# Convolution rows loaded once and copied shifted, with the background work drawn in sequence, in a four-layer network kernel

## The chip, the cores and the metric

The kernel runs on one core of a Trainium2 chip. The metric is device time in microseconds (us), the median of three executions. One further view, the profile, is of a single execution. Everything is f32.

The engines are named as in the profile: PE is TensorE's matmul side and PEld its weight load, DVE is VectorE, ACT is ScalarE, POOL is GpSimd, SP is SyncE. POOL, SP and ACT also issue DMA transfers, each on a queue of its own; sixteen DMA engines carry them all.

## The reference

The input x has shape 8 x 384 x 32 x 32 (images, channels, height, width). Four layers follow each other, all on the same shape.

- Layer 0: RMS norm over channels; a selective scan ("mamba") over the 1024 pixels of an image, forwards and backwards, on 384 channels with 16 states each; the gated result is projected and added, scaled, to x plus a local 3x3 depthwise branch with a sigmoid gate.
- Layer 1: a residual block with batch norm, a 1x1, a depthwise 3x3 and a 1x1 convolution; linear attention with 8 heads; layer norm and an MLP of 384 to 1536 to 384 with GELU.
- Layer 2: seven depthwise convolutions up to 13x13, some dilated, each with batch norm, summed.
- Layer 3: a 1x1 convolution with a residual, then a 13x13 depthwise convolution with batch norm plus a one-weight branch, and GELU.

The recurrence at the centre of layer 0 is

```
h[t] = exp(delta[t] * A) * h[t-1] + delta[t] * u[t] * B[t]      (per channel and state)
y[t] = sum over states of h[t] * C[t], plus D * u[t]
```

The seven kernels of layer 2 are merged into one 13x13 kernel per channel, and layer 3's last convolution is one 13x13 kernel too; both are computed by matmuls against Toeplitz matrices.

## The kernel before, in words

**Layers 0 and 1** work image by image. For each image b there are three generators, each of which issues a piece of work and then yields a number, its cost:

- `front(b)` (L554): norm, input projection (`in`, stored through `uz` tiles to `u_d` and `z_d`), local branch (`lc`), causal 1-D convolution (`c`, through `ut` loads), and the softplus that makes `dl` and `v` (Abs, Relu, Exp, Ln on ScalarE, sums on VectorE), written to DRAM for the scan.
- `scan(b)` (L678): 48 units, one for each direction, half image, group of 128 channels and group of 4 states. In a unit, ScalarE makes `da` by four exponentials (L754, two buffers), VectorE multiplies (`du`, L767, four buffers), runs the recurrence as one scan instruction (L774 or L777), and multiplies by C in the next unit (L691). PE then sums over states into `acc` (L693). After three channel groups of the backward direction the output projection (`op`) follows.
- `layer1(b)` (L840): the residual block (`h`, `dw`, `c2`), attention (`kv`, `q`, `rzb`, `pj`), norm, and the MLP (`mf`, GELU into `hm`, `mo`).

The main loop (L1036) runs `scan(b)`, and after each unit draws background work: `front(b + 1)`, `layer1(b - 1)`, and for the first two images preparations of weights (`fold`, L793, in image 0; `prepare`, L830, in image 1). It draws from whichever generator has the smallest drawn share of its declared total (108, 310, 30, 64), so that all of them advance side by side, and it draws until the drawn cost keeps pace with the units done. What is left after the last unit follows.

`prepare` merges the convolution kernels (L169) and expands them, with 64 DRAM to DRAM transfers on the POOL queue (L239, `tp_d<-g_d`, 672 KB each), into Toeplitz form; each pair of transfers is a step of cost 2.

The order of instructions on an engine isn't quite that of the program text. A scheduling framework places each instruction when its inputs and buffers are there in its own reckoning, by program order where several are ready, and fixes the queues of all engines before the kernel runs. Each engine then takes its queue in order. Tiles come from pools with a fixed number of buffers per tag: `t2` (128x512, 11 buffers), `s2` (128x512, 3, for the scan's small tiles), `a6` (128x3x512, 7), `w` (weights, 4), `im` (6), `bct` (4), `da` (2), `du` (4). PSUM has three `mm` tiles for short results, three `mo` for long ones, two `acc`.

**Layers 2 and 3** come when all images are done. `conv` (L282) treats the eight images of a channel row by row: a row of all images lies in DRAM with padding zeros between the images (`PADW`, 12; length `RL`, 364). For every four groups of four channels it loads the rows twice into `xt` (two buffers), into partitions 0 to 63 and, one element further, into 64 to 127 (L290 to L295), so that a matmul of 128 rows takes two taps at once. Each group has 28 matmul instructions (56 PE passes of half width) on PSUM tiles of six buffers. The Toeplitz tiles `tp` come by SP and ACT DMAs (L299 to L305) into three buffers. `put2` copies results out on VectorE and ScalarE by turns; between the two convolutions a 1x1 layer (L336 to L357) writes the padded rows of layer 3; `put3` applies GELU and stores the output.

Of the kernel before, what the change touches and what calls it, by code (L numbers as in the profile page):

```python
# [37 lines left out]
N_A6, N_T2, N_S2, N_W, N_IM = 7, 11, 3, 4, 6  # L38
TP = H * (KP // 2)
PADW = KS - 1  # L40
# [23 lines left out]
def tile_layers(  # L64
# [39 lines left out]
    RL = PADW + B * (W + PADW)  # L104
# [58 lines left out]
    def kernels(small, large):  # L163
# [65 lines left out]
        for g_d, t_d in ((g2_d, tp2_d), (g3_d, tp3_d)):  # L229
            for at in range(0, C // 2, NP):  # L230
                for q in range(2):
# [8 lines left out]
                    yield 2  # L240
# [8 lines left out]
    XL = RL - PADW // 2 - 6  # L249
    with tc.tile_pool(name="cw", bufs=1) as cwp, tc.tile_pool(name="cx", bufs=2) as cxp, tc.tile_pool(  # L250
# [31 lines left out]
        def conv(t_d, src_d, tag, put):  # L282
# [3 lines left out]
            xt = tp = None  # L286
            for g in range(NQ):
                if g % GB == 0:
                    xt = cxp.tile([P, 2 * GB, XL], FP, tag="xt", name=f"xt_{tag}_{g}")
                    for q in range(2):  # L290
                        src = bass.AP(
                            src_d.tensor, src_d[4 * g, 0, PADW - KS // 2 + q].offset,
                            [[RL, 2 * H], [2 * H * RL, 2 * GB], [1, XL]],
                        )
                        nc.gpsimd.dma_start(xt[2 * H * q : 2 * H * (q + 1)], src)  # L295
                ps = cps.tile([P, HALF], FP, tag="cv", name=f"cv_{tag}_{g}")
                if g % (GB // 2) == 0:
                    tp = toep[g // (GB // 2) % len(toep)]
                    for q in range(2):  # L299
                        for e in range(2):  # L300
                            lo = 2 * H * q + H * e
                            (nc.scalar if e else nc.sync).dma_start(
                                tp[lo : lo + H, :, e].rearrange("p g j t -> p g (j t)"),
# [32 lines left out]
        for t in range(H // 2):  # L336
# [3 lines left out]
            for m in range(NC):  # L340
# [10 lines left out]
                for r in range(2):  # L351
                    mid = xo[:, m, r, PADW:RL].rearrange("p (b w) -> p b w", w=W + PADW)[:, :, 0:W]
# [18 lines left out]
def _layers01(tc, nc, B, xv, x2_d, dram, ident, mean_w, eps5, eps6, one, half, minus1, vec, bns, bnt,  # L371
# [12 lines left out]
    with ExitStack() as ctx:  # L384
# [48 lines left out]
        zero = wp.tile([P, C + NC + 1], FP, tag="zero", name="zero")  # L433
        nc.gpsimd.memset(zero, 0.0)
        for i in range(2):
            for t, n in ((xn_d, IMG), (u_d, UL), (h_d, IMG)):
                pads = t[i].rearrange("(c p) i -> p c i", p=P)
                for c in range(NC):
                    for a in range(0, n, C):
                        e = min(n, a + C)  # L440
                        nc.gpsimd.dma_start(pads[:, c, a:e], zero[:, 0 : e - a])
# [21 lines left out]
        def s2(name):  # L463
            return sp.tile([P, HALF], FP, tag="s2", name=name, bufs=N_S2)

# [15 lines left out]
        def defer(n, fn):  # L481
            e = [n, fn]
            late.append(e)
            return e

        def force(e):
            if e in late:
                late.remove(e)
                e[1]()
# [64 lines left out]
        def front(b):  # L554
# [22 lines left out]
            for e in range(2):  # L577
                w = wtile(inproj_t[:, e * C : (e + 1) * C], f"win_{b}_{e}")
                for h in range(2):
                    for m in range(NC):  # L580
                        ps = psum(f"in_{b}_{e}_{m}_{h}")
                        dense(ps, w, m, xn[h])
                        t = t2(f"uz_{b}_{e}_{h}_{m}")
                        if e == 0:
                            nc.scalar.copy(t, ps)
                            nc.gpsimd.dma_start(uo[:, m, 3 + h * HALF : 3 + (h + 1) * HALF], t)
                        else:
                            nc.scalar.activation(t, ps, AF.Silu)  # L588
# [565 lines left out]
```

## Time and profile before

| what | us |
| --- | --- |
| median of 3 executions (6063.13 to 6068.56) | 6067.35 |
| the profiled execution's own time | 6068.56 |
| its span | 6066.8 |
| PE busy | 4850.3 (80%) |
| DVE busy | 3998.1 (66%) |
| ACT busy | 2852.0 (47%) |
| POOL busy | 1216.0 (20%) |
| start to the first scan multiply | 242.8 |
| scan of image 0 | 478.9 |
| scan of image 1 | 739.8 |
| scan of image 2 | 707.8 |
| scans of images 3, 4, 5, 6 | 556.5, 553.4, 550.6, 557.1 |
| scan of image 7 | 486.4 |
| layer 1 of image 7 alone | 391.8 |
| layers 2 and 3 | 801.6 |

A scan's stretch runs from its first L767 multiply to that of the next image. The page of the profile shows busy time per engine, the span in 40 slices with digits for tenths of busy time, the costliest groups of instructions with their mean duration and what ended the idle time ahead of them, and DMA issues. Other views answer for a stretch of time: busy time by engine, or who waited for whom.

### The profile page before, as it was taken

To read this page: it belongs to the slowest core of one execution; us is meant where nothing else is said; L and a number is where in the kernel's file an instruction comes from. 1 tells how busy PE (TensorE), PEld (TensorE's weight loads), DVE (VectorE), ACT (ScalarE), POOL (GpSimd) and SP (SyncE) were. 2 spreads that over 40 slices of the span, in tenths; PEclk is the share of its full clock that TensorE was granted. 3 is DMA by queue.
4 is the path that set the end of the run, shared out by engine and by line. 5 is a ranking of instruction groups with operands and counts; after the bars stand their busy time and mean duration, and the time that the engine had idled before them with its cause. 6 is when DMAs were issued, how large, how long until landed. Compare 5 with 4: busy or idle time off the path is not lost. (4 is left out here: it accounts for less than half of the span.)

```text
span 6066.8 us, 53234 instructions
## 1 busy us (share of the span) xinstructions
PE 4850.3 (80%) x19054; PEld 2142.6 (35%) x19054; DVE 3998.1 (66%) x2768; ACT 2852.0 (47%) x3941; POOL 1216.0 (20%) x1953
## 2 busy tenths in 40 slices
PE   3665546675479989898998999898978879798899
PEld 1121112222124324232333333242323324497488
DVE  0499995565674897998899789978989921000200
ACT  1555433443435755684577467556735513000211
POOL 4211111222122221212121121211110010211133
PEclk8676767787789989898999899898989979899999
DMA  8655554556473664567457556755663431598799
GB/s 284 202 181 178 181 187 135 167 171 186 139 224 117 192 203 147 170 203 211 143 181 212 157 183 184 213 151 165 199 171 111 142 95 47 111 221 192 220 217 196
DMA packets 429276, 1060.29 MB, mean 175 GB/s; under 512 B 61500, under 2 KB 111908, under 8 KB 429012
## 3 DMA queue, kind: packets, MB, share of 16 engines
q0 software_dynamic: 188640, 679.21, 39.0%
q1 hardware_dynamic: 210704, 354.31, 18.8%
q10 hardware_dynamic: 29668, 23.36, 1.6%
q8 instruction: 151, 2.47, 0.2%
q14 instruction: 113, 0.93, 0.1%
HBM read 807.16 MB, written 293.47 MB: 181 GB/s over the span
## 5 line engine op out<-in xcount | busy, mean ns | idle before, releaser
L754 ACT ACTIVATE da<-dlt,neg_a 128x512 f32<-128x512 f32 x1536 | 1005.2, 713 | 1061.3 <-DVE du L774 570.3
L767 DVE TENSOR_TENSOR du<-vr,bct 128x2048 f32<-128x2048 f32 x384 | 875.2, 2284 | 46.9 <-DMA vr<-v_d 41.0
L691 DVE TENSOR_TENSOR du<-du,bct 128x2048 f32<-128x2048 f32 x384 | 877.2, 2286 | 4.1 <-DVE xx L972 0.3
L777 DVE TENSOR_TENSOR_SCAN du<-da,du 128x2052 f32<-128x2052 f32 x192 | 848.8, 4427 | 13.9 <-ACT da L754 8.5
L774 DVE TENSOR_TENSOR_SCAN du<-da,du 128x2052 f32<-128x2052 f32 x192 | 848.0, 4426 | 8.5 <-ACT da L754 5.6
L693 PE MATMUL acc<-du,selt 128*32 128x512 f32 x3072 | 570.9, 687 | 324.2 <-DVE du L691 308.4
L1008 PE MATMUL mo<-hm,w 128*128 128x512 f32 x1152 | 568.0, 634 | 130.4 <-ACT hm L1006 129.3
L500 PE MATMUL mf<-ln,w 128*128 128x512 f32 x1152 | 552.3, 617 | 36.9 <-DMA w<-w_d 36.9
L1008 PEld LDWEIGHTS mo<-hm,w 128*128 128x128 f32 x1152 | 218.5, 200 | 474.8 <-issue 236.3
L500 PEld LDWEIGHTS mf<-ln,w 128*128 128x128 f32 x1152 | 214.9, 195 | 365.8 <-issue 326.2
L693 PEld LDWEIGHTS acc<-du,selt 128*32 128x32 f32 x3072 | 92.5, 115 | 681.8 <-DVE du L691 403.8
L312 PE MATMUL cv_b<-xt_b,toep 128*64 128x256 f32 x2688 | 304.5, 387 | 34.7 <-DMA xt_b<-xp_d 16.9
L509 PE MATMUL dw<-dw_i,t3b 96*32 96x512 f32 x1152 | 252.3, 784 | 99.0 <-DMA dw_i<-h_d 87.8
L312 PE MATMUL cv_a<-xt_a,toep 128*64 128x256 f32 x2688 | 302.9, 386 | 30.1 <-issue 24.2
L312 PEld LDWEIGHTS cv_b<-xt_b,toep 128*64 128x64 f32 x2688 | 291.6, 195 | 48.1 <-issue 33.5
L500 PE MATMUL in<-xn,win 128*128 128x512 f32 x576 | 284.2, 628 | 28.8 <-ACT uz L588 22.6
L312 PEld LDWEIGHTS cv_a<-xt_a,toep 128*64 128x64 f32 x2688 | 291.6, 195 | 41.1 <-issue 39.6
L754 ACT ACT_TABLE_LOAD x195 | 250.2, 1283 | 67.3 <-DVE du L777 41.1
L509 PE MATMUL lc<-lc_i,t 96*32 96x512 f32 x1152 | 188.4, 671 | 65.0 <-DMA lc_i<-xn_d 64.2
L1006 ACT ACTIVATE hm<-mf,biasf 128x512 f32<-128x512 f32 x192 | 129.9, 686 | 225.7 <-PE mf L500 224.3
L327 DVE COPY yt<-cv_a 128x256 f32<-128x256 f32 x48 | 20.4, 425 | 309.6 <-PE cv_a L312 309.6
L500 PE MATMUL h<-xx,c 128*128 128x512 f32 x288 | 143.6, 659 | 81.3 <-DMA xx<-x_d 81.3
(212 smaller groups left out, 6353.9 us busy)
## 6 DMA issues: line engine op xcount, KB each, us to landing
dlt<-dl_d SPq DMA_DIRECT2D x384, 256.0 KB, 5.3
vr<-v_d SPq DMA_DIRECT2D x384, 256.0 KB, 5.4
bct<-bc_d SPq DMA_DIRECT2D x256, 256.0 KB, 4.0
ut<-u_d POOLq DMA_DIRECT2D x192, 257.5 KB, 4.7
lc_i<-xn_d POOLq DMA_DIRECT2D x192, 228.8 KB, 4.6
dw_i<-h_d POOLq DMA_DIRECT2D x192, 228.8 KB, 4.2
tp_d<-g_d POOLq DMA_DIRECT2D x64, 672.0 KB, 9.4
w<-w_d POOLq DMA_DIRECT2D x64, 576.0 KB, 5.1
```

The lines of the kernel that those rows point to most:

```text
L312: nc.tensor.matmul(ps[2 * H * e : 2 * H * (e + 1), 0:BW], tp[:, 2 * (g % (GB // 2)) + e, :, :, t].rearrange("p c j -> p (c j)"), rhs, star ...
L327: nc.vector.tensor_copy(hold["t"][:, g % GB, :], ps)
L500: nc.tensor.matmul(ps, w[:, k, m * P : (m + 1) * P], rhs[k] if isinstance(rhs, list) else rhs[:, k, :], start=(k == 0), stop=(k == NC - 1),)
L509: nc.tensor.matmul(ps[32 * j : 32 * j + 32, :], lhs(j, i), rhs(j, i), start=(i == 0), stop=(i == taps - 1), skip_group_check=True,)
L691: nc.vector.tensor_mul(dv, dv, cct[:, 1:2, :].to_broadcast([P, 4, HALF]))
L693: nc.tensor.matmul(acc[32 * j : 32 * j + 32, :], selt, dv[:, j, :], start=False, stop=(r == NR - 1), skip_group_check=True,)
L754: nc.scalar.activation(da[:, SEG * j + 1 : SEG * (j + 1)], dlt[:, j, :], AF.Exp, scale=neg_a[:, 4 * c + j, r : r + 1],)
L767: nc.vector.tensor_mul(flat(1)[:, :, 0:HALF], vt, bct[r][:, 0:1, :].to_broadcast([P, 4, HALF]))
L774: nc.vector.tensor_tensor_scan(du[:, s], da[:, s], du[:, s], 0.0, ALU.mult, ALU.add)
L777: nc.vector.tensor_tensor_scan(du[:, s][:, ::-1], da[:, s][:, ::-1], du[:, s][:, ::-1], 0.0, ALU.mult, ALU.add)
L1006: nc.scalar.activation(hm, ps, AF.Gelu, bias=biasf[:, NC * i + f, :])
L1008: nc.tensor.matmul(acc[m], wb[:, f, m * P : (m + 1) * P], hm, start=(i == 0 and f == 0), stop=(i == FF // C - 1 and f == NC - 1),)
```

## The change

The diff has these parts.

1. In `conv`, the rows are loaded once, into one half of the partitions, and VectorE copies them, shifted by one element, into the other half. `flip` alternates which half is loaded, from one load to the next, and the Toeplitz tile's halves are placed to match.
2. `PADW` is 6 in place of 12, and `RL` 312 in place of 364. Two more elements stand at the end of a row.
3. The main loop draws from one sequence: all of `front(b + 1)`, then `fold` (image 0), then `layer1(b - 1)`. The declared totals are 94, 30 and 290, and the pace is counted over 48 steps in place of 47.
4. `prepare` is gone: its work is the end of `fold`, and the Toeplitz steps have cost 0.
5. `s2` is gone, its tiles come from `t2`, which has 10 buffers; `w` has 5 buffers and `bct` 5.
6. `uz`, `xr` and `fr` are `a6` tiles of three chunks, with one transfer each for three.
7. The residual of layer 1 is deferred by 0 in place of 1 steps, without the call that forces it ahead of the attention.
8. The tile of zeros is 512 wide in place of 388, so that the padding fills take 54 issues in place of 66.

```diff
-N_A6, N_T2, N_S2, N_W, N_IM = 7, 11, 3, 4, 6
+N_A6, N_T2, N_W, N_IM = 7, 10, 5, 6
-PADW = KS - 1
+PADW = KS // 2
-    RL = PADW + B * (W + PADW)
+    RL = PADW + B * (W + PADW) + 2
...
-                    yield 2
+                    yield 0
...
-    XL = RL - PADW // 2 - 6
+    XL = RL - 1
...
-                    for q in range(2):
-                        src = bass.AP(
-                            src_d.tensor, src_d[4 * g, 0, PADW - KS // 2 + q].offset,
-                            [[RL, 2 * H], [2 * H * RL, 2 * GB], [1, XL]],
-                        )
-                        nc.gpsimd.dma_start(xt[2 * H * q : 2 * H * (q + 1)], src)
+                    flip = g // GB % 2
+                    src = bass.AP(
+                        src_d.tensor, src_d[4 * g, 0, 0].offset,
+                        [[RL, 2 * H], [2 * H * RL, 2 * GB], [1, XL]],
+                    )
+                    half0, half1 = (xt[2 * H * e : 2 * H * (e + 1)] for e in (flip, 1 - flip))
+                    nc.gpsimd.dma_start(half0, src)
+                    nc.vector.tensor_copy(half1[:, :, 0 : XL - 1], half0[:, :, 1:XL])
...
+                            to = 2 * H * (q ^ flip) + H * e
                             (nc.scalar if e else nc.sync).dma_start(
-                                tp[lo : lo + H, :, e].rearrange("p g j t -> p g (j t)"),
+                                tp[to : to + H, :, e].rearrange("p g j t -> p g (j t)"),
...
-        zero = wp.tile([P, C + NC + 1], FP, tag="zero", name="zero")
+        zero = wp.tile([P, HALF], FP, tag="zero", name="zero")
...
                 for h in range(2):
+                    t = a6(f"uz_{b}_{e}_{h}")
                     for m in range(NC):
                         ps = psum(f"in_{b}_{e}_{m}_{h}")
                         dense(ps, w, m, xn[h])
-                        t = t2(f"uz_{b}_{e}_{h}_{m}")
                         if e == 0:
-                            nc.scalar.copy(t, ps)
-                            nc.gpsimd.dma_start(uo[:, m, 3 + h * HALF : 3 + (h + 1) * HALF], t)
+                            nc.scalar.copy(t[:, m, :], ps)
...
+                    if e == 0:
+                        nc.gpsimd.dma_start(uo[:, :, 3 + h * HALF : 3 + (h + 1) * HALF], t)
+                    else:
+                        nc.gpsimd.dma_start(zv[b][:, :, bass.ts(h, HALF)], t)
...
-                        t = sp.tile([P, 2, HALF], FP, tag="bct", name=f"bct_{b}_{d}_{h}_{e}", bufs=4)
+                        t = sp.tile([P, 2, HALF], FP, tag="bct", name=f"bct_{b}_{d}_{h}_{e}", bufs=5)
...
-        def prepare():
             large = lambda name: sp.tile([P, NC * C], FP, tag="w", name=name, bufs=N_W)
             yield from kernels(t2, large)
...
-                    res[h].append(defer(1, residual))
+                    defer(0, residual)
...
-                work.append([front(b + 1), 108, 0])
+                work.append((front(b + 1), 94))
+            if b == 0:
+                work.append((fold(), 30))
             if b > 0:
-                work.append([layer1(b - 1), 310, 0])
-            if b == 0:
-                work.append([fold(), 30, 0])
-            if b == 1:
-                work.append([prepare(), 64, 0])
-            need = sum(n for _, n, _ in work)
+                work.append((layer1(b - 1), 290))
+            need = sum(n for _, n in work)
+            steps = (cost for g, _ in work for cost in g)
             done = 0
             for i, _ in enumerate(scan(b)):
                 tick()
-
-                while work and done < need * (i + 1) / (rounds - 1):
-                    w = min(work, key=lambda w: w[2] / w[1])
-                    cost = next(w[0], None)
+                while done < need * (i + 1) / rounds:
+                    cost = next(steps, None)
                     if cost is None:
-                        work.remove(w)
-                        continue
-                    w[2] += cost
+                        break
                     done += cost
-            for w in work:
-                for _ in w[0]:
-                    tick()
+            for _ in steps:
+                tick()
```

## The prediction

> **What bounds the kernel now.** I began with the page's slices and its cost table, to see which engines are full and when.
>
> ```profile
> PE   3665546675479989898998999898978879798899
> DVE  0499995565674897998899789978989921000200
> PEclk8676767787789989898999899898989979899999
> DMA  8655554556473664567457556755663431598799
> L754 ACT ACTIVATE da<-dlt,neg_a 128x512 f32<-128x512 f32 x1536 | 1005.2, 713 | 1061.3 <-DVE du L774 570.3
> L767 DVE TENSOR_TENSOR du<-vr,bct 128x2048 f32<-128x2048 f32 x384 | 875.2, 2284 | 46.9 <-DMA vr<-v_d 41.0
> L691 DVE TENSOR_TENSOR du<-du,bct 128x2048 f32<-128x2048 f32 x384 | 877.2, 2286 | 4.1 <-DVE xx L972 0.3
> L774 DVE TENSOR_TENSOR_SCAN du<-da,du 128x2052 f32<-128x2052 f32 x192 | 848.0, 4426 | 8.5 <-ACT da L754 5.6
> ```
>
> A scan unit costs VectorE 2.28 + 2.29 + 4.43 = 9.0 us; 48 units are 432 us an image, and background work on VectorE brings it to some 510. I then cut the span where each image's scan begins (the time of its first L767) and asked for the busy time of every engine in each stretch.
>
> ```profile
> 243.00:722.00 479.00, 284.59 (x960) 85.45 (x960) 467.62 (x303) 268.16 (x386) 86.66 (x155) 0.68 0.55 182
> 722.00:1461.00 739.00, 448.38 (x1444) 161.33 (x1445) 488.38 (x340) 287.41 (x403) 143.82 (x223) 0.76 0.54 171
> 1461.00:2169.00 708.00, 564.67 (x1830) 208.84 (x1829) 498.67 (x323) 384.73 (x516) 137.22 (x229) 0.88 0.55 169
> 2169.00:2726.00 557.00, 495.14 (x1657) 180.48 (x1656) 490.20 (x316) 356.37 (x476) 112.87 (x193) 0.92 0.58 179
> 4873.00:5265.00 392.00, 316.95 (x889) 135.55 (x888) 40.41 (x55) 73.31 (x106) 59.76 (x80) 0.87 0.31 75
> 5290.00:5580.00 290.00, 271.89 (x2430) 263.17 (x2428) 18.27 (x43) 16.01 (x43) 45.74 (x64) 0.99 0.93 215
> 5745.00:6030.00 285.00, 269.29 (x2411) 260.12 (x2409) 0.00 (x0) 40.75 (x86) 105.23 (x128) 0.99 1.01 214
> ```
>
> Columns: stretch, length, then PE, PEld, DVE, ACT, POOL busy, granted clock, DMA share, GB/s. Image 0's scan is VectorE's alone (98%). Images 3 to 6 take 551 to 557 us with PE and VectorE both near 89%: nearly as good as VectorE's work allows. Images 1 and 2 take 739 and 708 with VectorE idle for 251 and 209 us: that is where time lies. The last image's MLP (392) and the convolutions (5265 on) are PE's; in the two convolution stretches PE idles 18 and 16 us while the DMA engines are full (0.93, 1.01).
>
> The waits tell what stops VectorE in images 1 and 2, and what does so later:
>
> ```profile
> DVE du L766 <- PE acc L693: 147.1, 7, 52.6
> DVE du L764 <- PE acc L693: 85.2, 15, 15.4
> ```
>
> The first line is of 722 to 2169 us, the second of 2169 to 4387. Both times the scan wants a `du` buffer (there are four) that PE's product still reads: PE is behind, with background work ahead of that product in its queue. In image 1 PE itself waits there on ScalarE (`in` for `uz` 22.6, `c` for `dw` 22.3, `den` for `lg` 19.8 us, once each), and ScalarE on the scan (`da` on `du` L777, 81.7 us in 897 to 1265). Three queues in order hold each other.
>
> **The Trainium skill.** "TensorE: Matmul & The Clock Gate" (The HAM clock gate) says a PE idle for a window of some 3.4 us falls to half clock; the trace agrees: 0.76 in image 1 and 0.92 to 0.94 once PE is dense. "DMA: Bandwidth & Descriptors" (Queues, rings and completion order) says that an engine consumes one queue's descriptors in ring order and alternates between queues; the trace agrees in part: beside the 5.8 MB zero fills of the first 160 us, a PE matmul waited up to 22.0 us for `lc_i`, whose median landing is 4.6. "VectorE: DVE Perf Modes" (The perf-mode tier table) is used below for the copy.
>
> **The change part by part.**
>
> *Convolution.* Per four channel groups the DMA engines carry 1408 KB of rows, 896 KB of kernels and 512 KB of output; rows fall to 64 x 8 x 311 x 4 B = 637 KB, so about 28% less. PE's floor stays: 112 matmuls, about 12.5 us. Added: 48 copies of 64x2480 f32. The page gives 1227 ns for a 2048-element f32 copy, so an estimate of 1.5 us at its doubled rate; bound above by the L767 row, 2480/2048 x 2.28 = 2.8. It is hidden behind 12.5 us of matmuls if landing (10.1 us for conv a, 8.0 for b, at full DMA) plus copy stays under 12.5: 11.6, or 12.9 at worst. With a quarter of the traffic gone I expect some 7 + 1.5. VectorE's `yt` copies queue behind it, covered by six PSUM buffers (about 19 us). The 34 us of PE idle shrink: **-20** (range -30 to +15).
>
> *Head.* The zero fills fall from 66 to 54 POOL issues of 0.53 us, ahead of `xi`: -6; 14% less of the 17.9 MB row fill at full DMA: -4. **-10** (-20 to +5). Batched `uz`, `xr`, `fr` transfers take fewer issues on POOL (20% busy), each starting later: nothing, as later loads are read from the order below; uncovered, a few us. The fifth `bct` and weight buffers relieve SP and POOL waits whose victims (`dlt`, `vr`) cost 80 us in the whole run, mostly at starts: nothing.
>
> *Order.* Background now runs front, then fold, then layer 1. Budgets of 94 and 290 against yields that sum to 108 and 310 leave 34 cost units after the last scan step. I took the listed order of both programs and summed, between successive scan products, the work on each engine: 0.43 us a 128x512 matmul pass (two each), 0.215 for a 32-column one, 1.28 a table load, durations of the rows for the rest. Totals per image are equal (PE 410, VectorE 510, ScalarE 365 against 380). Adding up the largest engine of every three units: before 632, 691 and 535 us for images 1, 2, 3; after 613, 598 and 598. By two units: 697, 753, 575; after 642, 619, 619. Before's images 2 and 3 took 708 and 557. A line through them puts the new steady image at 618 by three units, 594 by two; I take **605** for images 2 to 6.
>
> The listing shows why. PE has 47 us in two units at the image's end (undrawn MLP steps, `op`), 31 us of `in` at unit 2, and seven `dt` and eight `c2`/`kv` results before products 12 and 20. I counted PSUM results whose buffer (three) is freed by ScalarE two or more units ahead of PE's product: 7 in before's image 3, 35 in 2, 55 in 1; after 37 in each steady image, 15 of them three units ahead, where the fourth `du` buffer is used up. ScalarE has 95 us in units 12 to 17 (24 table loads, the softplus of both halves) against VectorE's 73. Images 2 to 6: 5 x 605 - (708 + 557 + 553 + 551 + 557 = 2926) = **+99**.
>
> *Toeplitz expansion.* The 64 `tp_d` transfers, spread over 760 to 1597 us before, become a run of 62 on POOL ahead of image 2's `xn_d` stores and `win` loads. 62 x 0.862 = 53 us of issue; 41 MB at 300 GB/s (which the head's busier slices reach) is 137, some 165 with SP's loads. Starting some 40 us into image 1, `win` lands near 205. PE then holds 12 `in`, 72 `lc` passes before product 8: VectorE stops after unit 11 (some 105 us) until about 265. So 510 + 160 + some 75 for later bursts = 745 against 740: **+5** (-80 to +80).
>
> *Ends.* Image 7's scan loses a little pressure: -12 by both sums. Fourteen-odd cost units of layer 1 move behind it to PE alone: +13. Image 0: sums equal, 0.
>
> Sum: -20 - 10 + 99 + 5 - 12 + 13 = +75 on the span of 6066.8; the profiled execution was 6068.6, the median 6067.4. **6140 us.**
>
> **Rivals.**
> - *The lag is absorbed (faster).* Three units of `du` slack smooth the bursts. By four units the sums are 555 before, 550 after, and before's image 3 did take 557. Then image 2 saves 150, and with -20 -10 +5 the run takes some 5890. The trace's near-full image 3 speaks for it; images 1 and 2, unsmoothed by the same buffers, against. It wins if a steady image stays under 585.
> - *Interlock.* Each deep PSUM result costs as between images 3 and 1: (229 - 46)/(55 - 7) = 3.8 us, so 46 + 30 x 3.8 = 160 over 510: 670 an image, 6065 + 425 = some 6480. Against it: image 1 also had the lowest clock.
> - *The queue run is cheap or long.* A POOL issue waiting on landings would put image 1 at 825 (6220); overlapped, at 665 (6060).
> - *The copy binds the convolutions:* 12.9 against 12.5, 48 x 0.4 = +20 in place of -20: 6180.
>
> **How the numbers follow.** Forecast with its queue and copy variants 0.54 (own range 6040 to 6260), interlock 0.16, absorbed 0.22, and 0.08 that the terms cancel. Within 0.2% (12 us, about what a measurement here can tell from no change) 0.06; a little of the cancelled case goes to either side: faster 0.24, slower 0.70. The range 5970 to 6340 leaves half of the absorbed and half of the interlock case out.
>
> **What would show it.** Right: images 2 to 6 equal at 590 to 625, VectorE idle some 100 us in each on `du` <- PE `acc`, granted clock under 0.90; in image 1 one long VectorE gap ending soon after `win` lands; PE over 96% in the convolutions, DMA share near 0.7. Wrong: steady images at 560 or less (absorbed), over 650 (interlock), `win` landing within 120 us of image 1's start, or PE waiting on VectorE L298.

## The result and the profile after

The changed kernel takes 6272.36 us (median of 4 runs, 6259.19 to 6276.8) against 6067.57 us for the kernel before on the same chip: a ratio of 1.0335, 95% interval 1.0317 to 1.0353. It is slower by 205 us. The forecast was 6140 (+75), range 5970 to 6340: the direction and the range hold, the size does not.

Cut at the same edges as in the prediction, in us, for the profiled executions (spans 6066.8 and 6272.3):

| stretch | before | after | change | forecast |
|---|---|---|---|---|
| head | 242.8 | 222.7 | -20 | -10 |
| scan of image 0 | 478.9 | 484.7 | +6 | 0 |
| image 1 | 739.8 | 770.0 | +30 | +5 |
| images 2 to 6 | 2925.4 | 3114.7 | +189 | +99 |
| image 7 | 486.4 | 514.6 | +28 | -12 |
| last image's layer 1 | 391.8 | 400.2 | +8 | +13 |
| layers 2 and 3 | 801.6 | 765.4 | -36 | -20 |

The page's slices and two rows of its cost table, the kernel after:

```profile
PE   4655407888788878987889788878878788999899
DVE  0599933897679767967798789778968960011211
PEclk8776557899789978897899889989989898999999
DMA  8654695446744664367435644664473362266577
L768 DVE TENSOR_TENSOR du<-vr,bct 128x2048 f32<-128x2048 f32 x384 | 874.6, 2285 | 28.2 <-DMA vr<-v_d 11.6
L599 DVE TENSOR_TENSOR lg<-lg,xn 128x512 f32<-128x512 f32 x48 | 33.1, 690 | 352.6 <-ACT lg L596 352.6
```

VectorE has sixes and sevens all through the steady images where it had eights and nines. An instruction of VectorE still takes what it took (2285 ns); the background's `lg` now has 353 us of idle time ahead of it. The stretches of the kernel after (length, then PE, PEld, DVE, ACT, POOL busy, granted clock, DMA share, GB/s):

```profile
707.40:1477.40 770.00, 482.48 (x1575) 177.19 (x1573) 494.46 (x348) 309.60 (x438) 159.26 (x242) 0.77 0.61 188
1477.40:2097.60 620.20, 525.91 (x1663) 191.91 (x1664) 492.67 (x314) 347.54 (x471) 103.05 (x173) 0.88 0.55 160
2097.60:2737.30 639.70, 525.68 (x1655) 191.13 (x1653) 492.79 (x314) 340.37 (x464) 103.92 (x174) 0.87 0.55 160
2737.30:3351.30 614.00, 514.80 (x1645) 189.33 (x1646) 492.43 (x315) 344.00 (x468) 103.42 (x173) 0.89 0.54 164
```

Image 2 lost its 708 us, and images 2 to 6 have 614 to 640 in place of some 555. The work is the same (VectorE 493 us); it idles some 121 to 147 us in each of those shown. The waits of the kernel after: first VectorE's in images 3 to 6 (2098 to 4592 us), then VectorE's in image 1 (707 to 1477), then POOL's between 700 and 960:

```profile
DVE xx L1013 <- PE mo L1004: 96.2, 4, 24.7
DVE du L767 <- PE acc L692: 82.6, 22, 6.8
DVE dl L665 <- ACT sp L660: 67.8, 12, 13.0
DVE xx L871 <- ACT c L868: 67.6, 23, 8.3
DVE lg L599 <- ACT lg L596: 57.7, 17, 8.9
DVE g L706 <- DMA zr<-z_d: 46.9, 5, 17.9
...
DVE lg L599 <- ACT lg L596: 171.2, 6, 134.6
...
POOL tp_d L239 <- DMA tp_d<-g_d: 114.7, 46, 5.5
```

Two things differ from what was forecast. The scan's own wait (`du` on `acc`, two rows, 118 us in four images) is 30 us an image, under a quarter of VectorE's idle time there, and before it was already 21. More than half of the idle time (289 of 524 us) lies in four kinds of background instruction (`xx` twice, `dl`, `lg`), which stand at the head of VectorE's queue and wait for ScalarE or TensorE with the scan behind them. The first row, `xx` on `mo`, is the end of layer 1's MLP; it costs 24 us an image, and 1.9 us in all four images of the kernel before. And a transfer that the waits quoted from before don't have, `zr`, keeps VectorE waiting up to 17.9 us. In image 1 the long gap is there as forecast (134.6 us, and `in` starts 230 us into the image; forecast: `win` at 205), and POOL itself stops 114.7 us, between one Toeplitz transfer and the next, for an earlier one to land. This wait is the program's: in the traces POOL's transfers use eight semaphores (111 to 118) in turn, and none is issued before the transfer eight ahead of it, which has the same semaphore, has landed. So at most eight of POOL's transfers are on their way at a time.

The convolutions, from the view of the tile `xt_a` of the kernel after (durations in ns: least, median, most):

```profile
L316 PE MATMUL cv_a<-xt_a,toep x2688: 377/386/702, 5506.9 to 5812.0; 128*64 128x256 f32 x192
L298 DVE COPY xt_a<-xt_a x24: 1444/1446/1449, 5505.4 to 5794.6; 64x2480 f32<-64x2480 f32 x24
```

The copy takes 1.45 us (median 1.50 in the second convolution; forecast 1.5), rows land in 5.6 to 8.3 us over both convolutions, TensorE is 96% busy at a DMA share of 0.66.

### The profile page after: what moved, and what is told of

It is laid out like the page before. It is cut to its first block, busy times and chain, and to the rows that moved or that the text cites. A ratio compares the mean times of both kernels' runs of the same rounds, so it can differ in the third digit from the quotient of the medians.

```text
span 6272.3 us, 52842 instructions
## 1 busy us (share of the span) xinstructions
PE 4976.3 (79%) x19054; PEld 2171.0 (35%) x19054; DVE 4075.4 (65%) x2816; ACT 2790.9 (44%) x3891; POOL 1105.0 (18%) x1733
## 5 line engine op out<-in xcount | busy, mean ns | idle before, releaser
L768 DVE TENSOR_TENSOR du<-vr,bct 128x2048 f32<-128x2048 f32 x384 | 874.6, 2285 | 28.2 <-DMA vr<-v_d 11.6
L692 PE MATMUL acc<-du,selt 128*32 128x512 f32 x3072 | 610.5, 696 | 272.1 <-DVE du L690 272.1
L1004 PE MATMUL mo<-hm,w 128*128 128x512 f32 x1152 | 554.5, 623 | 93.1 <-ACT hm L1002 90.4
L503 PE MATMUL lc<-lc_i,t 96*32 96x512 f32 x1152 | 254.9, 845 | 185.0 <-DMA lc_i<-xn_d 182.1
L494 PE MATMUL in<-xn,win 128*128 128x512 f32 x576 | 262.9, 613 | 138.9 <-DMA win<-in_inproj_t 129.3
L503 PE MATMUL dw<-dw_i,t3b 96*32 96x512 f32 x1152 | 266.1, 835 | 129.9 <-DMA dw_i<-h_d 104.0
L503 PE MATMUL c<-ut,t 128*32 128x512 f32 x768 | 248.0, 806 | 139.6 <-ACT dl L654 58.2
L599 DVE TENSOR_TENSOR lg<-lg,xn 128x512 f32<-128x512 f32 x48 | 33.1, 690 | 352.6 <-ACT lg L596 352.6
```

Of the source, the lines that this page charges most:

```text
L494: nc.tensor.matmul(ps, w[:, k, m * P : (m + 1) * P], rhs[k] if isinstance(rhs, list) else rhs[:, k, :], start=(k == 0), stop=(k == NC - 1),)
L503: nc.tensor.matmul(ps[32 * j : 32 * j + 32, :], lhs(j, i), rhs(j, i), start=(i == 0), stop=(i == taps - 1), skip_group_check=True,)
L692: nc.tensor.matmul(acc[32 * j : 32 * j + 32, :], selt, dv[:, j, :], start=False, stop=(r == NR - 1), skip_group_check=True,)
L768: nc.vector.tensor_mul(flat(1)[:, :, 0:HALF], vt, bct[r][:, 0:1, :].to_broadcast([P, 4, HALF]))
L1004: nc.tensor.matmul(acc[m], wb[:, f, m * P : (m + 1) * P], hm, start=(i == 0 and f == 0), stop=(i == FF // C - 1 and f == NC - 1),)
```

## The experiments

Ratios are to the kernel before on the same chip, with 95% intervals. The kernel before takes 6040 to 6075 us from chip to chip, so stretches of runs on different chips are compared with care: a few microseconds in an image mean nothing there.

### The convolution alone, and the order of drawing alone

First edit: the kernel before with only the changed `PADW`, `RL`, `XL`, row load and copy.

```diff
-PADW = KS - 1
+PADW = KS // 2
-    RL = PADW + B * (W + PADW)
+    RL = PADW + B * (W + PADW) + 2
...
+                    nc.vector.tensor_copy(half1[:, :, 0 : XL - 1], half0[:, :, 1:XL])
```

> The kernel before with the convolution change alone (one load, VectorE copy, six zeros). Theory (the gain of the convolutions is independent of the rest): layers 2 and 3 fall from 802 to some 765 us, everything ahead of them stays, total 6030 (6020 to 6040). Rival (part of the 36 us comes from where the convolutions start, with other pools and transfers still in flight): 6045 or more.

Measured: 6095.47 us, ratio 1.0094 (1.0078 to 1.0111): 55 us slower. Layers 2 and 3 fell to 765.2 us as in the full change, so the loss is in the scans of layers 0 and 1. There the traces show the instructions of VectorE, ScalarE and SyncE in the same order as before's, but for neighbours that start at nearly the same time. The rival's number came, but not for its reason: the convolutions kept their gain.

Second edit: the kernel before with only the new drawing loop, with `prepare` joined to `fold` and the Toeplitz steps free of cost.

```diff
-                    yield 2
+                    yield 0
...
-                    w = min(work, key=lambda w: w[2] / w[1])
-                    cost = next(w[0], None)
+                    cost = next(steps, None)
```

> The kernel before with the draw order of the changed one alone: front, then fold with the Toeplitz expansion, then layer 1, totals 94, 30, 290, Toeplitz steps of cost 0. Pools and transfers stay as before. Theory (the order is what costs): scans of images 2 to 6 at 610 to 640 us each, image 1 at 740 to 800, image 7 some 515, total 6300 to 6420. Rival (fewer small buffers and transfers batched by three are what costs): images 2 to 6 at 570 or less, total under 6180.

Measured: 6177.88 us, ratio 1.0225 (1.0203 to 1.0247). Images 2 to 6 take 612, 611, 605, 604, 606 us, 3039 together: near the forecast's 605 each, on the rows of before. Image 1 takes 726, image 7 500.5 (before 486). So the order alone is +138 us, where the prediction's terms for it (99 + 5 - 12 + 13) sum to +105.

### Budgets, and the Toeplitz run moved ahead

Edits to the changed kernel, each alone:

```diff
-                work.append((front(b + 1), 94))
+                work.append((front(b + 1), 108))
-                work.append((layer1(b - 1), 290))
+                work.append((layer1(b - 1), 310))
```

> The changed kernel with the declared totals equal to the real ones (108 and 310), so that no layer 1 work is left for the end of an image. Theory A (what costs is PE work bunched more than two or three units can take; the sum of the largest engine over three units falls from 598 to 567 an image): scans of images 2 to 6 at 585 to 605, total 6130 to 6190. Theory B (each PSUM result freed two or more units ahead costs, and their number rises from 37 to 59 an image): 650 or more an image, total over 6400. If neither holds: 6272.

Measured: ratio 1.0280 (1.0263 to 1.0297). Steady images 612 to 618 us, 3074 together: 5 to 8 us less an image than in runs of the changed kernel on two other chips (3115 and 3100). Work of the largest engine, summed over three units, had fallen from 598 to 567 us, and the images did not follow as theory A had it. Neither expectation held.

The waits of images 3 to 6 (2062 to 4523 us) are of use later. With nothing left over at the end of an image, the wait of `xx` on `mo` is gone from the list, `lg` falls to 30.0 us and `dl` to 24.9; `du` on `acc` rises from 118 to 292 us. The waits move from the background's instructions to the scan's, and an image takes nearly as long.

```diff
-                    yield 0
+                    yield 2
-                work.append((fold(), 30))
+                work.append((fold(), 108))
```

> The changed kernel with the Toeplitz transfers drawn as steps of cost 2 during the scan of image 0, in place of a run at its end. Theory (the run on the POOL queue holds the weights of image 2's projection back): image 1 falls from 770 to 620 to 650 us, the 129 us wait of PE for those weights is gone, image 0 grows by 10 to 25, total 6130 to 6165. Rival (image 1 is slow for another reason, as it was before with the transfers spread): image 1 stays over 720, total 6230 or more.

Measured: ratio 1.0342 (1.0321 to 1.0363), as the rival had it. The Toeplitz transfers now run from 578 to 900 us, and image 1 keeps 742 us. TensorE's waits in it (726 to 1469 us):

```profile
PE op L494 <- DMA wo<-in_outproj_t: 142.7, 1, 142.7
```

Image 0 takes 507 us (the changed kernel: 485), and the run of transfers ends at 900 us, where it ended at 915 in the changed kernel. The load behind it on POOL's queue is now `wo`, where it was `win`: the stall has changed its victim, not its size.

### Where the convolution's change costs the scans

First theory: fewer bytes in `x2_d` moved every later scratch tensor 2,555,904 bytes down in HBM, and transfers run slower there. The edit gives `x2_d` its old length with the new rows in it; the same for the changed kernel, and for the kernel before (which moves its tensors up by as much).

```diff
-    x2_d = dram.tile([C, H, RL], FP, tag="x2_d", name="x2_d")
+    n = C * H * RL
+    x2_d = dram.tile([n + C * H * (B * (KS // 2) + 4)], FP, tag="x2_d", name="x2_d")
+    x2_d = x2_d[0:n].rearrange("(c h r) -> c h r", c=C, h=H)
```

> The kernel before with the convolution's change alone, and the scratch tensor of the convolution's input (x2_d) given its old length, so that every scratch tensor behind it in HBM stands at the address it has in the kernel before (in the first run of the convolution's change alone they stood 2,555,904 bytes lower); rows keep the new pitch. No instruction is added or moved. Theory A: the 80 to 90 us that the scans lost with an unchanged order of instructions came from where the scratch tensors lie (landings of x_d<-xx 11.3 to 13.8 us, x_d<-fr 10.2 to 14.8, xx<-x_d 8.5 to 9.7). Then the scans come back, images 2 to 7 total 3390 to 3430 us, and the kernel is 0.993 to 0.997 of before. Theory B: it comes from the new rows themselves (writes of layer 1 into rows of the new pitch), or from the run. Then the ratio stays at 1.007 to 1.011.

> The changed kernel with the same length added to x2_d, so that most scratch tensors stand where the kernel before has them. Theory A (placement): 60 to 100 us are won in images 1 to 7, which would then stand at about 595 to 605 us each for the steady ones; ratio 1.018 to 1.024. Theory B (the order of the background alone): no change, ratio 1.032 to 1.035.

> The kernel before with 2,555,904 bytes more in x2_d, unused: the same instructions, scratch tensors behind it that much higher. Theory A (placement as such decides): a difference of either sign of over 0.3%, up to 1.5%. Theory B: 0.998 to 1.002.

Measured: 1.0092 (1.0077 to 1.0107), 1.0319 (1.0302 to 1.0337) and 0.9989 (0.9981 to 0.9997). Placement is not it; the theory fell. But these runs led to the answer. Layer 1 writes its result into `x2_d` in runs of 32 values, 128 bytes, one for each channel and row (the `x_d<-xx` transfers, 3 for each image and half). In the convolution-alone run with the old length, the view of that one line, cut into short stretches of time, gives the landings of three writes at a time (least, median, most, in us; the line above, where shown, has the times of issue). In this order: second half of image 2, first half of image 3, second half of image 3, first half of image 4:

```profile
L1025 POOL DMA_DIRECT2D x_d<-xx x3: 1154/1162/1202, 2756.1 to 2758.5; - x3
DMA to landing us min/median/max: 9.0/14.8/20.3
...
L1025 POOL DMA_DIRECT2D x_d<-xx x3: 1154/1170/1195, 3196.0 to 3202.4; - x3
DMA to landing us min/median/max: 6.3/7.3/7.8
...
DMA to landing us min/median/max: 5.0/6.1/8.3
...
DMA to landing us min/median/max: 13.4/16.8/20.0
```

Image 3 lands in 6 to 7 us, its neighbours in 15 to 17; image 7 is the only other quick one (median 6.0 over both halves), and the other images have medians of 13 to 21. In the changed kernel the same two are quick (medians 7.0 and 5.9, the others 17.5 to 20.5). With six zeros, and if the tensor itself starts at a multiple of 32, image b's run starts at byte 24 + 152 b of a row, and rows are 1248 bytes apart: a multiple of 32 for b = 3 and b = 7, and for no other image. In the kernel before it is 48 + 176 b + 1456 h for row h, a multiple of 32 in every second row of every image, and the median landing is 11.2 us (9.8 in its run with room added). So the second theory: a 128-byte write that does not start at a multiple of 32 bytes is slow, and with six zeros three images of four are written so wholly. The two quick images have the same pitch of rows as the others, so the pitch by itself is not the reason.

The edit that tests it puts eight zeros in place of six (and eight ahead of the first image): every run then starts at a multiple of 32 bytes. It was made in the convolution-alone kernel, in the kernel before (rows still loaded twice, no copy), and in the changed kernel.

```diff
-PADW = KS // 2
+PADW = 8
-    RL = PADW + B * (W + PADW) + 2
+    RL = PADW + B * (W + PADW)
-    XL = RL - 1
+    XL = RL - 2
-                        src_d.tensor, src_d[4 * g, 0, 0].offset,
+                        src_d.tensor, src_d[4 * g, 0, PADW - KS // 2].offset,
```

> The kernel before with the convolution's change, but eight zeros between images in place of six and eight ahead of the first: then each run of 32 values that layer 1 writes into x2_d starts at a multiple of 32 bytes. Theory A (start of the 128-byte writes): in the run with six zeros the writes x_d<-xx of images 3 and 7, the only ones whose runs start at a multiple of 32 bytes, landed in 5 to 6 us and the others in 16 to 21; in the kernel before, where half of the rows do, in 10. Now all land in 5 to 7 us, the scans take what they take in the kernel before or less, and the ratio is 0.985 to 0.996. Theory B (the row pitch as such, or the copies): 1.007 to 1.011 again.

> The kernel before, rows still loaded twice and not copied, with eight zeros in place of twelve between images: every run written starts at a multiple of 32 bytes. Theory A: x_d<-xx from 10 to 5 to 7 us, scans 20 to 80 us shorter; with 8% less in the convolutions' row loads the ratio is 0.983 to 0.996. Theory B: 0.996 to 1.002, from the loads alone.

> The changed kernel with eight zeros in place of six. Theory A: images 2 to 6 come from 614 to 640 down to 590 to 610 each, which is what the drawn order alone gave on the rows of the kernel before (604 to 612) or a little less; ratio 1.008 to 1.022. Theory B: images as they were, ratio 1.030 to 1.035.

Measured: 0.9878 (0.9862 to 0.9895), 0.9901 (0.9883 to 0.9920), 1.0168 (1.0148 to 1.0187). All three as the second theory said. Layers 2 and 3 have a part in it: of the convolution-alone kernel's gain over before (72 us), some 47 lie there (750 us, against 796 in before's run with room added), and 766 us in the second run, with the rows still loaded twice, is 30 less than 796. What the writes cost is seen better against six zeros: from the changed kernel with room added to the one with eight zeros, the time ahead of layers 2 and 3 falls by 69 us.

The landing of all 48 writes in the convolution's kernel with eight zeros, same view:

```profile
DMA to landing us min/median/max: 4.3/5.9/11.1
```

The medians of the other two are 6.1 and 6.7 us.

What slow writes do to the scans is seen in the waits of images 2 to 7: first the convolution's change with six zeros (1450 to 4933 us), then with eight (1454 to 4843):

```profile
DVE du L772 <- DMA vr<-v_d: 58.1, 14, 20.8
DVE xn L575 <- ACT rstd L555: 50.2, 8, 23.1
PE h L505 <- DMA xx<-x_d: 91.4, 6, 21.1
```

```profile
DVE xn L573 <- ACT rstd L553: 17.5, 7, 11.3
DVE du L770 <- DMA vr<-v_d: 11.9, 10, 3.9
PE h L503 <- DMA xx<-x_d: 53.3, 6, 13.0
```

Transfers that follow the writes come late. The stores `x_d<-fr`, whose tensor has the same layout in both kernels, go out on the same queue (KB each, median us to landing; six zeros, then eight):

```profile
x_d<-fr POOLq DMA_DIRECT2D x48, 256.0 KB, 14.0
x_d<-fr POOLq DMA_DIRECT2D x48, 256.0 KB, 4.7
```

With six zeros, the 34 of them that were issued while a row write was on its way have a median of 15.9 us, the other 14 of 3.7. Layer 1's load `xx` has to wait for these stores (POOL 67.4 us in images 2 to 7 with six zeros, 29.3 with eight), and TensorE's `h` for that load. And as only eight transfers can be on their way, POOL also holds back loads that have nothing to do with the writes (`ut`, 25.9 us with six zeros). The loads `vr` come on another queue, SP's; why they are late was not followed up, and a wait for `dlt` (22.4 us, once) that only the run with eight zeros has gives part of the 46 us back. Images 1 to 7 take 4224 us with six zeros, 4140 with before's twelve (the run with room added) and 4132 with eight.

In the changed kernel the load of the next image's rows, `xi`, waits on POOL for the writes to land, since both use `a6` buffers; first six zeros (1477 to 4592 us), then eight (1450 to 4489):

```profile
POOL xi L554 <- DMA x_d<-xx: 77.5, 4, 24.1
POOL xi L554 <- DMA x_d<-xx: 29.5, 4, 7.6
```

The `zr` wait of images 3 to 6 goes from 46.9 us to 3.2.

### What is left of the order's cost

With eight zeros the changed kernel's steady images (first three of five) and those of before's order with the convolution alone:

```profile
1449.70:2058.60 608.90, 522.14 (x1656) 189.04 (x1649) 492.48 (x315) 343.75 (x468) 103.49 (x173) 0.89 0.51 165
2058.60:2665.90 607.30, 520.49 (x1671) 188.62 (x1669) 492.29 (x314) 343.42 (x468) 103.51 (x173) 0.89 0.52 166
2665.90:3270.40 604.50, 520.76 (x1647) 189.46 (x1648) 492.46 (x315) 343.79 (x468) 103.34 (x173) 0.89 0.52 166
```

```profile
2149.00:2703.90 554.90, 493.57 (x1657) 179.97 (x1650) 489.95 (x314) 355.56 (x476) 112.94 (x193) 0.93 0.58 180
2703.90:3254.30 550.40, 491.84 (x1662) 180.86 (x1661) 491.69 (x315) 357.31 (x480) 113.02 (x193) 0.93 0.58 183
```

The same VectorE work, 55 us more. TensorE runs as many instructions too, but is busy for 521 us in place of 493, at a granted clock of 0.89 in place of 0.93. Whether the lower clock is a cause of the lateness or comes of TensorE's waiting, no run separates. The first test puts before's drawing loop and `prepare` back into the changed kernel (with six zeros), and keeps its pools and joined transfers:

```diff
-            steps = (cost for g, _ in work for cost in g)
...
+                    w = min(work, key=lambda w: w[2] / w[1])
```

> The changed kernel with before's way of drawing the background (the furthest behind next, Toeplitz steps at their old cost, the layer-2 weights prepared beside image 1): what stays of the change is the convolution, the pools and the joined transfers. If the draw order is what costs the scans: images 2 to 6 at 553 to 575 us each, near the run of the convolution's change alone, ratio 1.000 to 1.010. If the pools or the joined transfers (two t2 rows, one a6 tile for two halves) cost it: images 2 to 6 at 600 and more, ratio 1.025 to 1.035.

Measured: ratio 1.0034 (1.0023 to 1.0045); images 3 to 6 take 559 to 567 us. In before's order the pools and joined transfers cost nothing. Beside the convolution alone on the same chip (1.0092) they gain 0.6%; in the profiles images 1 and 2 (1427 us together, against 1462) and the head (217 against 229) carry it. The profiled execution was the fastest of its 20 (6036.82, median 6066.2), so these stretches flatter it.

The second test: a fifth `du` buffer, with its room taken from one `w` and one `bct` buffer, beside a control with only these two taken away.

```diff
-N_A6, N_T2, N_W, N_IM = 7, 10, 5, 6
+N_A6, N_T2, N_W, N_IM = 7, 10, 4, 6
...
-                du = sp.tile([P, 4 * SEG + 1], FP, tag="du", name=f"du_{b}_{i}", bufs=4)
+                du = sp.tile([P, 4 * SEG + 1], FP, tag="du", name=f"du_{b}_{i}", bufs=5)
```

> Control for the next run: the changed kernel with eight zeros, and one buffer fewer each for the weights (w, 5 to 4) and for bct (5 to 4), the numbers of the kernel before. Both theories: steady images 604 to 616 us, ratio 1.014 to 1.024 of before.

> The control with a fifth du buffer in the room so won. Theory A (the four du buffers are what a late product of TensorE stops VectorE by, the step that the prediction named for the steady images): by the order of the program the largest engine's work in every three units falls from 598 to 567 us, waits du <- acc shrink by more than half, and a steady image takes 570 to 592 us; ratio 0.985 to 1.005. Theory B (VectorE stops on the background's own instructions, xx, dl, lg and xx <- c, which stand ahead of the scan's in its queue): images at 598 to 615 us, these waits as before, ratio 1.010 to 1.022.

Measured: 1.0124 (1.0108 to 1.0140) and 1.0133 (1.0117 to 1.0148). Steady images 605 to 614 us with the fifth buffer. VectorE's waits of images 3 to 6 in that run:

```profile
DVE xx L1013 <- PE mo L1004: 95.3, 4, 23.8
DVE dl L665 <- ACT sp L660: 70.1, 12, 14.5
DVE du L767 <- PE acc L692: 61.5, 16, 6.8
```

`du` on `acc` (L767) falls by a quarter (82.5 in the control) and nothing is won: theory B. The prediction's step "where the fourth `du` buffer is used up" does not hold for this kernel; one buffer more does not free the scan. It was not tried with the full totals, where the wait on `acc` is the largest.

The third test moves the two background instructions with removable waits later in VectorE's queue, in the changed kernel with eight zeros (the second run of the pair delays `deltas` by three):

```diff
-                    defer(1, local)
+                    defer(4, local)
...
-                    defer(1, deltas)
+                    defer(2, deltas)
```

> The changed kernel with eight zeros, with two kinds of the background's VectorE instructions put into its queue later: lg (local) after five scan units in place of two, dl (deltas) after three in place of two. Nothing else is changed. Theory B (VectorE loses its time by standing at the head of its queue before such an instruction whose ScalarE operand is late): waits lg <- lg and dl <- sp of images 3 to 6 fall from 115 us to under 50, and a steady image from 608 to 580 to 597 us; ratio to before 1.000 to 1.012. Rival (ScalarE and TensorE are late themselves, and whichever VectorE instruction stands first takes the wait): the waits move to du <- acc and du <- da, images at 600 to 615, ratio 1.011 to 1.019.

> As the run above, with dl after four scan units. Theory B: a little below it (575 to 597 us an image). Rival: 600 to 615.

Measured: 1.0099 (1.0077 to 1.0121) and 1.0120 (1.0093 to 1.0147). Images 598 to 605 and 597 to 607 us. The waits of the first, images 3 to 6:

```profile
DVE du L775 <- ACT da L755: 51.0, 8, 12.1
DVE lg L599 <- ACT lg L596: 32.7, 8, 6.4
DVE dl L665 <- ACT sp L660: 22.4, 13, 4.0
```

These two waits fall from 115 us to 55, and `du` on ScalarE's `da` rises from 25 to 51. An image wins some 6 us where 15 had gone from the two rows. The first run's ratio lies in theory A's range, its waits and images do not. The rival has the better of it, and the waits with the full totals say the same: an instruction at the head of the queue mostly shows that ScalarE or TensorE is late, and when it is moved another takes the wait. The largest row, `xx` on `mo` (97.1 us here), was moved by neither run, so what a later place for it alone would win is open. The idle time lies in the first half of an image. Stretches of 12 scan units of image 4, the changed kernel with eight zeros:

```profile
2665.90:2843.30 177.40, 149.07 (x474) 51.88 (x478) 125.16 (x86) 94.09 (x119) 37.31 (x61) 0.89 0.60 187
2843.30:3018.40 175.10, 142.03 (x465) 43.23 (x458) 128.97 (x85) 107.59 (x154) 44.89 (x83) 0.79 0.59 192
3018.40:3151.10 132.70, 119.84 (x420) 52.36 (x419) 123.19 (x85) 66.14 (x104) 7.12 (x11) 0.96 0.33 113
3151.10:3270.40 119.30, 109.81 (x296) 41.99 (x296) 115.15 (x62) 75.98 (x92) 14.03 (x19) 0.95 0.49 157
```

The first two quarters take 352 us for 254 us of VectorE work and lose 98 us of the 112 lost in the image; the last two lose 14. By the program, the first half draws the whole of `front` and the first 84 of layer 1's 310 cost units, behind what the image before left over. Neither TensorE nor ScalarE is full over either of these quarters (at most 84% busy). So chains between the engines are the likely cause of the lateness; that is argued, not shown, and which link would have to be shortened was not found.

### Versions faster than both

Before's drawing, the convolution's change with eight zeros, and `prepare` drawn beside image 0, whose scan leaves TensorE free, in place of image 1. The first keeps before's pools, the second has the change's pools and joined transfers.

```diff
             if b == 0:
                 work.append([fold(), 30, 0])
-            if b == 1:
                 work.append([prepare(), 64, 0])
```

> The run with the convolution's change and eight zeros, with the layer-2 weights also prepared beside image 0 in place of image 1; order of drawing as in the kernel before. The largest engine's work in every three units falls from 691 to 535 us in image 2 and rises from 632 to 665 in image 1. If image 2 then takes 555 to 580 us and image 1 stays under 790: ratio 0.962 to 0.980. If the preparation's transfers stop image 1 as they did in the changed kernel (over 800 us), nothing is won over the run with eight zeros alone.

> The changed kernel with eight zeros, before's way of drawing the background, and the layer-2 weights prepared beside image 0: the pools and the joined transfers of the change are kept. If these two are worth what the earlier pair of runs showed (1.0034 against 1.0094, 35 us, on rows of six zeros), this run is 20 to 40 us below the best so far (0.9727): ratio 0.965 to 0.970. If that gain came from image 1 and 2 only, which the preparation beside image 0 already empties: 0.970 to 0.976.

Measured: 5878.94 us, ratio 0.9727 (0.9709 to 0.9745), and 5856.63 us, ratio 0.9655 (0.9629 to 0.9681), on two chips where the kernel before takes 6045 and 6075 us. Both lie in the range expected; in time the second is 22 us below the first. The first three images of the second:

```profile
211.60:878.60 667.00, 274.74 (x950) 91.02 (x954) 479.13 (x348) 257.24 (x380) 135.83 (x204) 0.63 0.61 199
878.60:1490.40 611.80, 487.01 (x1617) 176.55 (x1618) 488.75 (x305) 342.06 (x460) 102.09 (x173) 0.87 0.53 170
1490.40:2036.70 546.30, 484.49 (x1659) 180.10 (x1658) 493.67 (x315) 351.64 (x476) 104.01 (x173) 0.94 0.59 184
```

Images 0 to 2 take 1825 us against 1927 in the table of the kernel before: image 0 pays 188 us for the preparation, images 1 and 2 save 290.

## Why the prediction was right or wrong

- **Convolution (-20): the step that failed.** Inside layers 2 and 3 the gain was larger (-36): the landings fell to some 7 us, as expected, but nearly all of the 34 us of TensorE's idle time in the two convolutions went, where 20 had been put down. But the sum gave the new row layout no price outside them. Every image writes 1.5 MB into those rows during the scans, and where the runs start decides how long that takes. On rows of six zeros the convolution's change costs 84 us over images 1 to 7 (4224 against 4140), and made alone it slows the whole kernel by 55 us, where -20 was forecast. No step named these writes.
- **Steady images (605): right in number for the order, by luck.** The order alone takes 608 on average (3039 / 5), and so does the changed kernel with eight zeros (3039). Of the 90 us by which images 2 to 6 exceed the forecast, 14 are the order's, 61 the writes' (the changed kernel with room added, 3100, less the one with eight zeros, 3039), and the last 15 lie between two runs of the same order on two chips. But the number came from a line through two points, and the sums by three units behind it did not rank the kernels: 598 and, with a fifth `du` buffer, 567 gave the same 604 to 614 us on rows of eight zeros. They told before's even image 3 (535) from an uneven one, and no more. The reason given, that the fourth `du` buffer is used up, is not what the runs show.
- **Image 1 (+5): right in mechanism, +30 in size.** The long VectorE gap and its end came much as worked out, and the stall of POOL on landings that a rival had is there (114.7 us) without its 825 us. With eight zeros the image takes 741 us, with six zeros and room added 748, so some 7 of the 30 go with the rows; the 22 between 748 and 770 lie between two runs of the same order on two chips.
- **Image 7 (-12): wrong in sign.** The order alone brings 500.5 us, the changed kernel with eight zeros 506.8. The window sums that gave -12 are the same that failed to rank the steady images.
- **Head (-10), ends (+13), copy.** -20, +8, and 1.45 us: right in direction, small. The head of the kernel before alone ranged from 232 to 243 us in two runs of its instructions, so half of that gain may be chance.
- **Rivals.** The lag was not absorbed (wins under 585: no image was). The interlock's 670 was not reached. The copy did not bind. The expected sign of wrong, "over 650", did not come, though image 3 (640) and image 6 (625.2) lie outside the 590 to 625 of the signs of right. Of these, the clock (0.87 to 0.89) and TensorE's 96% came; VectorE's idle "some 100 us on `du` <- `acc`" did not: it was 30 an image on that and the rest on background instructions.
- **Slips in the working.** The 637 KB of rows are 622 in the units of the other two figures, which leaves the 28% as it is. The -4 for the row fill asks for some 640 GB/s; at the 300 GB/s used elsewhere the 2.6 MB less would be some 8 us. The wait of 22.0 us on `lc_i` is the weight load's, the matmul's is 21.1.

The Trainium skill bears on the write. "DMA: Bandwidth & Descriptors" (Specifications) says that below 512 bytes a transfer does a read-modify-write, and its section "How a descriptor splits into AXI transactions" counts from multiples of 256 bytes. "Collectives: The Full Stack" (Rules for kernel authors) wants collectives' buffers at multiples of 32 bytes so that no read-modify-write is needed. The 512 does not separate the runs here, which are all of 128 bytes. They agree with the 32 for plain stores: 6 us against 13 to 21, though half of the quick ones do not start at a multiple of 64. That a read-modify-write is what makes the others slow is the pages' explanation; the trace shows only the time.

## What to carry to other kernels

When a layout changes, price its writers as well as its readers: for every store into the changed tensor, work out at which byte each contiguous run now starts. Where runs are as short as the 128 bytes here, try rows padded so that all start at a multiple of 32 bytes, even if that is two values more. An edit that leaves the instruction order alone can still slow other stages: stores on the same queue landed late behind the late writes (15.9 us against 3.7), and the loads that waited for them with these. And test a change's parts one by one on the chip: here the part forecast as a small gain lost 0.9%, and with two more zeros it gained 1.2%, of which two thirds lie in the convolutions themselves. A wait on an engine's list need not be what to remove: here the waits moved from row to row while the images kept nearly their length.

## What the runs showed of the hardware that was not expected

- 128-byte stores: median landing 5.9 to 6.7 us where all start at multiples of 32 bytes, 9.8 to 11.2 where half do, 13 to 21 where none does (256 KB transfers, the same bytes).
- Moving most scratch tensors by 2.4 MiB up or down in HBM changed nothing that matters: 0.9989, and 1.0092 beside 1.0094.
- The convolution's stages took 765 us with rows of 38 values an image and 750 with 40, though the second moves 5% more; TensorE's busy time fell from 736 to 720 us, the median matmul from 386 to 381 ns.
